# Factor rows, normalised rows and blocks of x in natural order of the contraction

## The chip, the cores and the metric

The kernel runs on one core of a Trainium2 chip. The metric is the device time of one execution in microseconds (us), as a median of runs. The engines are TensorE (PE, with its weight loads as PEld), VectorE (DVE), ScalarE (ACT), GpSimd (POOL) and SyncE (SP), whose queue issues nearly all DMAs.

## The reference

Eight sequences of 1024 tokens with 1024 features go through a cross attention over 64 memory rows and then a linear layer whose weight is a sum of eight factors; both have a layer norm before them and a residual.

```python
x = x + xattn(_layernorm(x), ctx)            # x: (8, 1024, 1024), ctx: (8, 64, 1024)
x = x + ffn(_layernorm(x), factors, bias)    # factors: (8, 1024, 1024), bias: (1024,)

scores = einsum('bsd,bmd->bsm', h, ctx) / sqrt(D)    # masked, then softmax over m
readout = einsum('bsm,bmd->bsd', attn, ctx)          # xattn
mixed = einsum('btd,rde->bte', h, factors)           # ffn
mixed = mixed / sqrt(8) + bias
```

All is float32.

## The kernel before

**Groups.** The 8192 tokens are cut into 16 groups of 512, each four row tiles of 128 tokens (`x` tiles, 128 x 1024). A group has two pairs of tiles; `q` and `h` number them, tile 2h + q.

**The weight.** The sum over the eight factors is made once, on TensorE. `load_stack e i c h` loads, for two of four blocks `j` of 256 rows of the weight, 16 rows of each of the 8 factors into a tile of 128 partitions: partition 8k + r holds row k of factor r, 4 KB long. A load is 512 KB; there are 64 of them, 33.5 MB, one for each `e` (4), `i` (2), `c` (2), `h` (2) and half tile `j`. `add_stack` multiplies them by a matrix `stack[i]` of 128 x 32 with a one where partition and output row belong together, so that the eight factors are summed; `i = 0` and `i = 1` are accumulated in one bank, each filling 16 of the 32 output rows of a block (line 718). `take_sums` copies the sums out of PSUM to the seven weight tiles `b11`, `t1` and so on, in chunks of 128 contraction rows numbered 2e + c (four to a tile; e and e + 2 go to different ones). `subtract_factors` and `combine_factors` make the further tiles of a Strassen-like scheme from them.

**The contraction order.** Chunk 2e + c of the 1024 features holds, from each of the four blocks `a` of 256, 32 of them. Before, a feature's index is read as (a, k, e, i, c) with k of 16, e of 4, i and c of 2: a chunk takes features with a step of 16 (over k) and a step of 2 (over i). The helpers `by_chunks`, `in_order` and `in_blocks` write that order as access patterns, and all that is contracted follows it:

- `normalize` (line 568) writes the normalised rows `h` from `x` with two activations of 512 elements, one for each c. In group 0 the result is in the order of chunks, in the others in blocks of 256 with the order inside each.
- `relayout` (line 585) moves, by 16 DMAs of 64 KB, block a of 32 tokens to partitions 32a and on, and `transpose_rows` (line 594) transposes that by squares of 32 x 32 on VectorE to `hT`, the stationary operand of the products. Group 0 is transposed on TensorE instead (`transpose_h_pe`).
- `load_blocks` (line 318) loads x a second time in such blocks, `transpose_blocks` (line 390) transposes them for the scores with two VectorE instructions of 128 x 256 for each e, one for each c. Groups 0 and 1 are transposed on TensorE (`transpose_x_pe`), with columns in steps of 8.
- `centre_memory` (line 287 and on) centres the memory rows, in the order of chunks with two activations, except for the first sequence.

**The products.** `product` (line 626) and `part` (line 676) are the matmuls of the linear layer, `give` (639) and `give_part` (690) add their results from PSUM to `x` on VectorE, `add_bias` (575) adds the bias on GpSimd, `read_out` (501) and `residual` (509) are the attention's output, `norm_sums` and `norm_squares` (537, 548) the statistics of the second norm. `store` (701) writes a tile out.

**Order.** Every engine works its instructions in the order in which the program writes them, and that is written by hand: the table START lists the steps of the beginning, among them all `load_stack` and `add_stack`, mixed with the work of groups 0 and 1; the table LOOP is then run for every group, with p, g, n and m standing for the group before, this one, the next and the one after. Tiles of the large kind come from ten buffers (`bigs`), taken and given back in the order of the table: factor loads, `xb`, `xT`, `h`, `hb` and `hT` share them. Eight PSUM banks are shared in the same manner. A factor load waits on SP's queue until the buffer that it takes has been given back by its reader, and whatever is behind it in SP's queue waits with it.

The load itself and the matrices that sum what it brings are these lines:

```python
src = factors.rearrange("r (j k e i c) n -> e i c j k r n", j=NA, e=NS, i=2, c=2)[e, i, c]
for j in range(2):
    nc.sync.dma_start(f[:, j], src[2 * h + j])
```

Of the kernel before, what the change touches and what calls it, by code (L numbers as in the profile page):

```python
# [10 lines left out]
F32 = mybir.dt.float32  # L11
BF16 = mybir.dt.bfloat16
AF = mybir.ActivationFunctionType
ALU = mybir.AluOpType
AX = mybir.AxisListType
# [91 lines left out]
def kernel(  # L107
# [17 lines left out]
    nc = tc.nc  # L125
    P = 128
    B, S, D = x.shape
    M = mem.shape[1]
    R = factors.shape[0]
    Q = 32  # L130
    NA = P // Q
    DA = D // NA
    NC = DA // Q
    KH = NC // 2
    NS = NC // 2
# [11 lines left out]
    const = ctx.enter_context(tc.tile_pool(name="const", bufs=1))  # L147
# [25 lines left out]
    ident = const.tile([P, P], F32, name="ident")  # L173
# [1 line left out]
    neghalf = const.tile([P, 4], F32, name="neghalf")  # L175
    nc.gpsimd.memset(neghalf, -0.5)

    stack = [const.tile([P, 2 * P // R], F32, name=f"stack{i}") for i in range(2)]
    for i in range(2):
        nc.vector.memset(stack[i], 0.0)  # L180
        nc.vector.tensor_reduce(
            stack[i].rearrange("p (k i) -> p i k", i=2)[:, i], ident.rearrange("p (k r) -> p k r", r=R), AX.X, ALU.add
        )

# [47 lines left out]

    st = {}

    def by_chunks(ap):

        return ap.rearrange("p (k e i c) -> p e c k i", e=NC // 2, i=2, c=2)

    def in_order(ap):
        return ap.rearrange("p (e c k i) -> p e c k i", e=NC // 2, c=2, i=2)

    def in_blocks(ap):

        return ap.rearrange("p (a e c k i) -> p e c a k i", a=NA, e=NC // 2, c=2, i=2)

    def constants():

        room = bigs.take("mask", [P, 2, 8 * P], "mask_room")  # L250
        st["mask"] = room[:, 0, : B * M].bitcast(mask.dtype)[:, : B * M], room[:, 1, : B * M], room[:B, 0, 4 * P : 5 * P]
        nc.scalar.dma_start(st["mask"][0], mask.rearrange("b m -> (b m)").partition_broadcast(P))
        for h in range(P // M):
            nc.scalar.dma_start(mask8[:, h], mask)
# [25 lines left out]
    def centre_memory(g: int):  # L280


        b = g // GPB
        m = st["mem", b]
        mc = bigs.take(("memc", b), [P, 2 * D], f"memc_{b}")[:, :D]
        msum = small.tile([P, 1], F32, tag="msum", name=f"msum_{b}")
        nc.scalar.activation(mc[:M], m[:M], AF.Copy, accum_out=msum[:M])
        mneg = small.tile([P, 1], F32, tag="mneg", name=f"mneg_{b}")
        nc.gpsimd.tensor_scalar_mul(mneg[:M], msum[:M], -1.0 / D)
        if b == 0:  # L290
            nc.scalar.activation(mc[:M], m[:M], AF.Identity, bias=mneg[:M])
        for c in range(2 if b else 0):
            nc.scalar.activation(
                in_order(mc)[:M, :, c], by_chunks(m)[:M, :, c], AF.Identity, bias=mneg[:M]
            )
        st["memc", b] = mc

# [85 lines left out]
    def transpose_blocks(g: int, h: int, e: int):  # L383

        xb = st["xb", g, h]
        if e == 0:
            st["xT", g, h] = bigs.take(("xT", g, h), [P, NC, 8 * Q], f"xT_{g}_{h}")
        xT = st["xT", g, h]
        for c in range(2):
            nc.vector.transpose(  # L390
                xT[:, 2 * e + c].rearrange("p (t j) -> p t j", j=Q),
                xb.rearrange("p t (k e i c) -> p e c t k i", e=NC // 2, i=2, c=2)[:, e, c],
            )
        if e == NC // 2 - 1:
            bigs.back(("xb", g, h))

# [160 lines left out]
    def normalize(g: int, q: int, h: int):  # L557
        rstd, nb = st["norm", g, q]
        if h == 0:
            st["h", g, q] = bigs.take(("h", g, q), [P, 2, D], f"h_{g}_{q}")  # L560
        src, dst = st["x", g, 2 * h + q], st["h", g, q][:, h, :]
        for c in range(2):
            fr = by_chunks(src)[:, :, c]
            if g == 0:
                to = in_order(dst)[:, :, c]
            else:
                to, fr = in_blocks(dst)[:, :, c], fr.rearrange("p e (a k) i -> p e a k i", a=NA)
            nc.scalar.activation(  # L568
                to, fr, AF.Identity, bias=nb[:, h : h + 1], scale=rstd[:, h : h + 1]
            )  # L570

    def add_bias(g: int, q: int, k: int, eng=nc.gpsimd):

# [131 lines left out]
    def load_stack(e: int, i: int, c: int, h: int):  # L705

        f = st["f", e, i, c, h] = bigs.take(("f", e, i, c, h), [P, 2, D], f"f_{e}_{i}_{c}_{h}")
        src = factors.rearrange("r (j k e i c) n -> e i c j k r n", j=NA, e=NS, i=2, c=2)[e, i, c]
        for j in range(2):
            nc.sync.dma_start(f[:, j], src[2 * h + j])  # L710

# [104 lines left out]
```

## Time and profile before

| | us |
|---|---|
| median of 3 runs | 1001.92 (1001.43 to 1004.05) |
| the profiled execution | 998.04 |
| its span, first to last instruction | 996.1 |
| TensorE busy | 937.4 |
| VectorE busy | 729.6 |
| ScalarE busy | 463.4 |
| GpSimd busy | 248.4 |

The profile is of one execution. Busy times are the time in which an engine runs at least one instruction; a mean duration times a count can be more, as instructions overlap. A line of the waits says who waited for whom, how long in total, how often, and the longest. A line of the groups says line, engine, operation, output and inputs, shapes and count, then busy time and the mean duration in ns, then the idle time before and what ended it. The DMA share of a window is the mean busy share of the 16 DMA engines.

### The profile page before, as it was taken

Reading aid. Unit: us, or ns where it says so; the run is one execution under the profiler, and the core shown is the slowest. Engines: PE = TensorE matmul, PEld = TensorE weight load, DVE = VectorE, ACT = ScalarE, POOL = GpSimd, SP = SyncE. Lnnn points to the kernel's source line nnn. Section 1 sums busy time; section 2 is a strip of 40 time slices with the busy share of each in tenths; the row PEclk is TensorE's granted clock in tenths of the full one; section 3 lists DMA queues with packets and bytes.
Section 4 is the critical chain, followed back from the end, with each engine's and each line's share of the span. In section 5 each row is a group of like instructions: output and inputs, shape, how many; then the busy total and the mean of one; then the engine's idle time right before and its main releaser. Section 6 shows DMA issues by size and latency. Waiting matters only on the chain.

```text
span 996.1 us, 12006 instructions
## 1 busy us (share of the span) xinstructions
PE 937.4 (94%) x3785; PEld 578.0 (58%) x3785; DVE 729.6 (73%) x1565; ACT 463.4 (47%) x848; POOL 248.4 (25%) x355
## 2 busy tenths in 40 slices
PE   5777766999999999999999999999999999999998
PEld 4322221566666666657575667665666757576666
DVE  4412143978797979797978889697979697888785
ACT  4745000167373727454655537363746456454200
POOL 0100020025141413223242313150423324232321
PEclk9979889999999999999999999999999999999999
DMA  9998899674847465565747484747565574742312
GB/s 277 255 269 225 205 224 234 149 191 141 197 148 167 138 166 159 167 151 161 188 135 198 127 191 151 176 140 164 155 171 148 155 189 135 193 131 77 105 69 85
DMA packets 98175, 167.07 MB, mean 168 GB/s; under 512 B 12864, under 2 KB 72384, under 8 KB 98112
## 3 DMA queue, kind: packets, MB, share of 16 engines
q1 hardware_dynamic: 97632, 165.20, 63.3%
q10 hardware_dynamic: 480, 1.12, 0.4%
q8 instruction: 29, 0.48, 0.2%
q14 instruction: 34, 0.28, 0.1%
HBM read 101.25 MB, written 33.55 MB: 135 GB/s over the span
## 4 chain that ended last, share of the span: by engine, by line
PE 80%; DMA 14%; SPq 3%; DVE 1%; issue 1%; ACT 0%; ACTq 0%; DVEq 0%
PE yu L626 30%; DMA f<-in_L_ffn_factors_dram 12%; PE ro L501 6%; PE y4u L676 5%; PE scT L433 5%; PE y3u L676 5%; PE y2u L676 5%; PE y5u L676 5%; SPq L585 3%; PE y4v L676 3%; PE y5v L676 3%; PE y3v L676 3%; PE y2v L676 3%; PE sum L718 2%; PE y3z L676 1%; PE y2z L676 1%
## 5 line engine op out<-in xcount | busy, mean ns | idle before, releaser
L575 POOL TENSOR_TENSOR x<-x,bias_bc 128x512 f32<-128x512 f32 x128 | 168.1, 1327 | 274.4 <-DVE x L639 209.5
L626 PE MATMUL yu<-b,hT 128*128 128x512 f32 x256 | 117.4, 602 | 10.0 <-DVE hT L594 8.2
L537 ACT ACTIVATE junkz<-x 128x1024 bf16<-128x1024 f32 x64 | 67.7, 1058 | 119.9 <-DVE x L509 117.1
L626 PE MATMUL yu<-t,hT 128*128 128x512 f32 x256 | 115.1, 592 | 0.0
L626 PE MATMUL yu<-t,s 128*128 128x512 f32 x256 | 115.0, 592 | 0.0
L594 DVE STREAM_TRANSPOSE hT<-hb 128x1024 f32<-128x1024 f32 x60 | 74.0, 1235 | 54.8 <-DMA hb<-h 50.8
L509 DVE SCALAR_TENSOR_TENSOR x<-ro,rden,x 128x512 f32<-128x512 f32 x128 | 89.9, 746 | 32.8 <-PE ro L501 32.8
L568 ACT ACTIVATE h<-x,nb,rstd 128x512 f32<-128x512 f32 x128 | 95.8, 820 | 16.2 <-PE sum L718 11.9
L364 ACT ACTIVATE junk<-x,nmean 128x1024 bf16<-128x1024 f32 x56 | 64.3, 1148 | 47.7 <-POOL nmean L335 46.7
L639 DVE SCALAR_TENSOR_TENSOR x<-yu,x 128x512 f32<-128x512 f32 x128 | 82.7, 677 | 5.0 <-PE yu L626 5.0
L626 PEld LDWEIGHTS yu<-b,hT 128*128 128x128 f32 x256 | 49.1, 193 | 61.8 <-issue 46.8
L718 PE MATMUL sum<-f,stack 128*32 128x512 f32 x256 | 57.1, 687 | 27.4 <-DMA f<-in_L_ffn_factors_dram 27.4
L390 DVE STREAM_TRANSPOSE xT<-xb 128x256 f32<-128x256 f32 x224 | 80.7, 417 | 1.2 <-issue 1.2
L626 PEld LDWEIGHTS yu<-t,s 128*128 128x128 f32 x256 | 48.5, 190 | 48.9 <-issue 46.8
L548 ACT ACTIVATE junky<-x,zm 128x1024 bf16<-128x1024 f32 x64 | 73.5, 1148 | 7.1 <-POOL zm L335 4.8
L626 PEld LDWEIGHTS yu<-t,hT 128*128 128x128 f32 x256 | 48.6, 190 | 47.6 <-issue 45.9
L501 PE MATMUL ro<-mem,eT 64*128 64x512 f32 x256 | 66.4, 628 | 2.6 <-ACT eT L490 2.6
L335 POOL TENSOR_SCALAR zm<-zs 128x2 f32<-128x2 f32 x28 | 6.3, 225 | 240.2 <-ACT junkz L537 240.2
L352 ACT ACTIVATE junk<-x 128x1024 bf16<-128x1024 f32 x56 | 59.0, 1053 | 13.4 <-DMA x<-in_x_dram 12.4
L690 DVE SCALAR_TENSOR_TENSOR x<-y3u,x 128x256 f32<-128x256 f32 x64 | 26.6, 416 | 47.3 <-PE y3u L676 44.3
L433 PE MATMUL scT<-xT,memT 128*64 128x256 f32 x512 | 58.8, 382 | 0.7 <-ACT memT L309 0.7
L718 PEld LDWEIGHTS sum<-f,stack 128*32 128x32 f32 x256 | 10.4, 118 | 70.1 <-DMA f<-in_L_ffn_factors_dram 44.9
(147 smaller groups left out, 1598.3 us busy)
## 6 DMA issues: line engine op xcount, KB each, us to landing
x<-in_x_dram SPq DMA_DIRECT2D x64, 512.0 KB, 4.1
f<-in_L_ffn_factors_dram SPq DMA_DIRECT2D x64, 512.0 KB, 13.8
out_dram<-x SPq DMA_DIRECT2D x64, 512.0 KB, 3.2
hb<-h SPq DMA_DIRECT2D x480, 64.0 KB, 2.0
xb<-in_x_dram SPq DMA_DIRECT2D x112, 256.0 KB, 7.1
mem<-in_ctx_dram SPq DMA_DIRECT2D x14, 256.0 KB, 5.4
mem<-in_ctx_dram ACTq DMA_DIRECT2D x2, 256.0 KB, 6.1
bias_bc<-in_L_ffn_bias_dram ACTq DMA_DIRECT2D x1, 512.0 KB
```

What stands on the lines that cost most here:

```text
L390: nc.vector.transpose(xT[:, 2 * e + c].rearrange("p (t j) -> p t j", j=Q), xb.rearrange("p t (k e i c) -> p e c t k i", e=NC // 2, i=2, c= ...
L433: nc.tensor.matmul(ps[ts(h, M), : 2 * P], mT[:, c, :], st["xT", g, h][:, c, :], start=(c == 0), stop=(c == NC - 1),)
L501: nc.tensor.matmul(ps, eT[ts(h, M), q, :], m[ts(h, M), ts(n, H)], start=True, stop=True)
L509: nc.vector.scalar_tensor_tensor(xt, st.pop(("ro", g, q, n, h)), rden[:, k : k + 1], xt, ALU.mult, ALU.add)
L548: nc.scalar.activation(junk, st["x", g, 2 * h + q], AF.Square, bias=nmean[:, h : h + 1], accum_out=ss[:, h : h + 1])
L568: nc.scalar.activation(to, fr, AF.Identity, bias=nb[:, h : h + 1], scale=rstd[:, h : h + 1])
L575: eng.tensor_add(xt, xt, bias_bc[:, ts(k % 2, H)])
L594: nc.vector.transpose(st["hT", g, q][:, h].rearrange("p c (t j) -> p t c j", j=Q), hb[:, h].rearrange("p t (c i) -> p t c i", i=Q),)
L626: nc.tensor.matmul(ps, lhs[:, c, :], wq[right][:, c, :], start=(first and c == 0), stop=(c == KH - 1), skip_group_check=True,)
L639: nc.vector.scalar_tensor_tensor(xt, st["y", g, q, key], ISR, xt, ALU.mult, ALU.add)
L676: nc.tensor.matmul(ps, lhs[:, c, :], right[:, c, :], start=(first and c == 0), stop=(c == 1), skip_group_check=True,)
L718: nc.tensor.matmul(st["sums", e, c][n][ts(j, Q)], stack[i], st["f", e, i, c, j // 2][:, j % 2, ts(n, H)], start=(i == 0), stop=(i == 1),)
```

## The change

The contraction is put in natural order: chunk 2e + c takes 32 consecutive features from each block of 256. A feature's index is read as (a, e, c, i, k), k innermost. A factor load then takes 16 consecutive rows of each of the 8 factors instead of 16 rows that are 16 apart; rows of the same factor lie next to each other in memory, those of different factors 4 MiB apart as before. `normalize` becomes one activation of 1024 elements (with the order of chunks written for group 0 alone), `transpose_blocks` one VectorE instruction of 128 x 512 for both c, `centre_memory` one activation. The two matrices `stack[0]` and `stack[1]` become two views of one tile of 48 columns, 16 columns apart. The tables START and LOOP are not touched, nor are tile sizes and buffers.

```diff
-    stack = [const.tile([P, 2 * P // R], F32, name=f"stack{i}") for i in range(2)]
-    for i in range(2):
-        nc.vector.memset(stack[i], 0.0)
-        nc.vector.tensor_reduce(
-            stack[i].rearrange("p (k i) -> p i k", i=2)[:, i], ident.rearrange("p (k r) -> p k r", r=R), AX.X, ALU.add
-        )
+    stacks = const.tile([P, 3 * P // R], F32, name="stacks")
+    nc.vector.memset(stacks, 0.0)
+    stack = [stacks[:, (1 - i) * P // R : (3 - i) * P // R] for i in range(2)]
+    nc.vector.tensor_reduce(stack[0][:, : P // R], ident.rearrange("p (k r) -> p k r", r=R), AX.X, ALU.add)
...
-        for c in range(2 if b else 0):
+        else:
             nc.scalar.activation(
-                in_order(mc)[:M, :, c], by_chunks(m)[:M, :, c], AF.Identity, bias=mneg[:M]
+                mc[:M].rearrange("p (n a w) -> p n a w", a=NA, w=Q),
+                m[:M].rearrange("p (a n w) -> p n a w", a=NA, w=Q),
+                AF.Identity,
+                bias=mneg[:M],
             )
...
-        for c in range(2):
-            nc.vector.transpose(
-                xT[:, 2 * e + c].rearrange("p (t j) -> p t j", j=Q),
-                xb.rearrange("p t (k e i c) -> p e c t k i", e=NC // 2, i=2, c=2)[:, e, c],
-            )
+        nc.vector.transpose(
+            xT[:, ts(e, 2)].rearrange("p c (t j) -> p t c j", j=Q),
+            xb[:, :, ts(e, 2 * Q)].rearrange("p t (c w) -> p t c w", w=Q),
+        )
...
-        for c in range(2):
-            fr = by_chunks(src)[:, :, c]
-            if g == 0:
-                to = in_order(dst)[:, :, c]
-            else:
-                to, fr = in_blocks(dst)[:, :, c], fr.rearrange("p e (a k) i -> p e a k i", a=NA)
-            nc.scalar.activation(
-                to, fr, AF.Identity, bias=nb[:, h : h + 1], scale=rstd[:, h : h + 1]
-            )
+        if g == 0:
+            dst = dst.rearrange("p (n a w) -> p a n w", n=NC, a=NA)
+            src = src.rearrange("p (a n w) -> p a n w", n=NC, a=NA)
+        nc.scalar.activation(dst, src, AF.Identity, bias=nb[:, h : h + 1], scale=rstd[:, h : h + 1])
...
-        src = factors.rearrange("r (j k e i c) n -> e i c j k r n", j=NA, e=NS, i=2, c=2)[e, i, c]
+        src = factors.rearrange("r (j e c i k) n -> e i c j k r n", j=NA, e=NS, i=2, c=2)[e, i, c]
```

More of the change, by code (lines that the diff above doesn't have):

```diff
@@ L235 @@
     st = {}
[L237 to L246, printed above, removed]
     def constants():
```

## The prediction

> **What bounds the kernel now.** I read the page first (busy time, the 40 slices, the chain of work that ended last), then the DMA shares by window, then the waits of TensorE, then the groups of the lines that the diff touches.
>
> ```profile
> span 996.1 us, 12006 instructions
> PE 937.4 (94%) x3785; PEld 578.0 (58%) x3785; DVE 729.6 (73%) x1565; ACT 463.4 (47%) x848; POOL 248.4 (25%) x355
> ...
> PE   5777766999999999999999999999999999999998
> ...
> PE 80%; DMA 14%; SPq 3%; DVE 1%; issue 1%; ACT 0%; ACTq 0%; DVEq 0%
> ```
>
> TensorE is idle for 996.1 - 937.4 = 58.7 us, and the slices show where: each is 25 us, and only the first seven or eight and the last are below 9. From 200 us on it is the bound. The chain has DMA as its second term, ACT and DVE with nearly nothing.
>
> The windows (length, then busy time of PE, PEld, DVE, ACT, POOL, the granted clock, the DMA share, GB/s) tell the two kinds of load apart:
>
> ```profile
> 2.00:4.00 2.00, 0.00 (x0) 0.00 (x0) 0.00 (x0) 0.38 (x1) 0.00 (x0) 1.00 0.98 363
> 10.00:12.00 2.00, 2.00 (x11) 2.00 (x10) 1.97 (x5) 0.88 (x2) 0.00 (x0) 1.00 1.02 416
> 60.00:70.00 10.00, 9.14 (x56) 3.96 (x48) 2.26 (x4) 6.31 (x12) 0.00 (x0) 0.88 1.03 268
> 150.00:160.00 10.00, 6.50 (x18) 1.69 (x18) 0.00 (x0) 0.58 (x1) 1.11 (x1) 0.83 1.03 239
> 250.00:300.00 50.00, 49.51 (x207) 32.46 (x206) 43.15 (x94) 27.97 (x52) 14.07 (x21) 1.00 0.65 171
> ```
>
> Before about 12 us the queue holds rows of x: 128 consecutive rows of 4 KB in each load (the first factor load is issued at 9.1 us behind six of them). They go at 363 to 416 GB/s. From then on it holds factor loads, of the same 4 KB pieces, and with the engines just as full (share 1.03) they bring 269, 268, 266 at 50 to 80 us and 239, 239, 240 at 140 to 170 us, mean 253.5. So the size of the pieces is not what makes them slow; the addresses are what differs. By the shapes, the 128 pieces of a factor load come from 8 factors, 4 MiB apart, and in each from 16 rows, 64 KiB apart.
>
> ```profile
> by line: PE yu L626 30.0%; DMA f<-in_L_ffn_factors_dram 12.3%; PE ro L501 5.8%; PE y4u L676 5.4%; PE scT L433 5.1%; PE y3u L676 5.1%; PE y2u L676 5.1%; PE y5u L676 4.9%; SPq L585 2.8%; PE y4v L676 2.7%; PE y5v L676 2.7%; PE y3v L676 2.7%; P
> ...
> PE sum L718 <- DMA f<-in_L_ffn_factors_dram: 27.4, 20, 3.9
> PE tp L405 <- DMA x<-in_x_dram: 10.9, 2, 9.7
> PE yu L626 <- DVE hT L594: 8.2, 1, 8.2
> PE ro L501 <- ACT eT L490: 2.6, 1, 2.6
> PE yu L626 <- ACT b L733: 1.8, 1, 1.8
> ```
>
> Factor loads carry 12.3% of the chain, 0.123 x 996.1 = 122.5 us, all before 172 us, and are the longest wait of TensorE. The start is bound by them; the rest by TensorE.
>
> **The loads.** The bytes (64 issues of 512 KB), the piece (4 KB) and the issues stay; the 16 rows of a factor become neighbours, 64 KB in one run, while the 8 factors stay 4 MiB apart. The trace has no such pattern; its neighbours are x (one run of 512 KB) and the factor loads of before. Upper end: they become like x at its best, 416 / 253.5 = 1.64 times the rate. Lower end: the same step the other way, 253.5 / 1.64 = 155 GB/s, since one can't exclude from the trace that the 64 KiB steps are what keeps the eight factors' rows out of each other's way. Other factors' rows are still mixed into each load, so I don't take x's full rate but the geometric middle between it and no change, 1.28 times (325 GB/s). The 122.5 us then shrink by 122.5 x (1 - 1/1.28) = 26.8 us. Not all arrives: faster loads expose what runs beside them. In the start TensorE waits 27.4 us for factors, and 8.2 + 2.6 + 1.8 = 12.6 us for things that don't get faster (the transposed rows behind the two relayouts, each 16 issues on SP's queue at some 0.6 us; the softmax weights; the copied sums), and factor loads need one of ten buffers that TensorE frees. I take 27.4 / 40.0 = 0.7 of it: 19 us.
>
> [...]
>
> **The normalised rows.** Before, two activations of 512 per tile, each with strided reads:
>
> ```profile
> L568 ACT ACTIVATE h<-x,nb,rstd 128x512 f32<-128x512 f32 x128 | 95.8, 820 | 16.2 <-PE sum L718 11.9 <-POOL nb L554 4.4
> L548 ACT ACTIVATE junky<-x,zm 128x1024 bf16<-128x1024 f32 x64 | 73.5, 1148 | 7.1 <-POOL zm L335 4.8
> L390 DVE STREAM_TRANSPOSE xT<-xb 128x256 f32<-128x256 f32 x224 | 80.7, 417 | 1.2 <-issue 1.2
> L594 DVE STREAM_TRANSPOSE hT<-hb 128x1024 f32<-128x1024 f32 x60 | 74.0, 1235 | 54.8 <-DMA hb<-h 50.8 <-issue 2.0 <-PE memTp L306 2.0
> ```
>
> After, 64 of 1024. Nearest is the square's pass over 1024 with a bias, 1148 ns (1058 for the sum's pass, at most 2 x 820 = 1640): 64 x 1.15 = 73 us against 128 x 0.82 = 105, some 32 us less in durations, 22 less in busy time. Beside TensorE it is worth nothing: its windows add up to 53.4 us of idle time before 200 us, so 5.3 of the 58.7 come later, 4.6 of these in the last 46 us, where ACT does nothing. On the path it counts in the start alone, where group 1's four activations (2.95 us) stand ahead of a relayout; two take 2.3. Two such places give 1.3 us at most; I take 1. Group 0's rows, in four tiles, write runs of 32 elements instead; between 1148 and 1640 ns that is no loss against 1640.
>
> **The transposes of x.** 224 of 256 elements become 112 of 512. A line through 417 ns at 256 and 1235 at 1024 gives 690 at 512 (bounds: half of 1235, 618, and twice 417, 834): 112 x 0.69 = 77 us instead of 93, 16 us off DVE. What hides it is the same: after 200 us TensorE never waits for DVE for more than the 0.8 and 0.7 us of combined rows. If that cover were thinner the longer single instruction could delay an eviction by 0.27 us; the products' banks show no such wait, so nothing is counted.
>
> **The rest.** The centred memory rows lose one activation in each of seven batches: hidden under TensorE, nothing. The stack matrices lose one memset and one reduce (0.09 + 0.29 us on DVE before 2 us, where DVE waits for x until 9.6): nothing. The matrices are still 32 columns wide, slid along a common tile, so all 256 sum matmuls stay; TensorE loses and gains no instruction. No wait is added and no issue is moved past another: the tables START and LOOP are the same.
>
> **Sum.** The profiled execution took 998.04 us, 996.1 of span and 1.9 around it: 998.0 - 19 - 1 = 978. The median, 1001.92, lies 3.9 above that execution, so 982 as a median. At x's rate: 47.8 x 0.7 = 33.5, so 967.
>
> **The rivals.** *The factors' 4 MiB sets the rate.* The loads stay near 250 GB/s, and what remains is the 1 us of activations: 1001 us. For it: both 8 factors and 64 KiB separate the loads from x, and only the second goes. Against it: the rate was not one number (268 at 60 us, 239 at 150), with the same factor distance in every load, so something else in the addresses matters too.
>
> *Neighbouring rows of eight factors get in each other's way.* Place: the factor loads from 13 to 172 us. [...] If that costs as much as I expect it to bring, the rate is 253.5 / 1.28 = 198 GB/s, the 122.5 us grow by 34, nothing hides them because they are the chain already, and the median becomes 1035; with the full step 122.5 x 0.64 = 78, 1079. It decides as soon as the rate falls under 247 GB/s (3 us more on the chain). For it: the only measured pattern with several factors is slow. Against it: x shows that neighbouring rows as such are fast.
>
> *A faster load that gives nothing.* If buffers and relayouts held the start fully, the DMA share would be well under 1 there. It is 1.02 to 1.04 in nearly every window to 170 us except 90 to 110 and 120 to 130 (0.60 to 0.82), so this can only eat a part, the 0.3 already taken off.
>
> **How the numbers follow.** Faster loads 0.52, no effect on them 0.09, slower loads 0.39: the rows of x speak for the first, that the loads keep the factors' distance leaves much room for the last. About 0.3% (3 us) is what a measurement of this kernel can tell from no change, so the same three chances stand for faster, same and slower. The forecast is the likeliest case, 982; its own range is 964 to 996. To leave out no more than 2 in 10 the range must reach through no change into slower loads, past its middle at 1035: 962 to 1042.
>
> **What would show it.** Right: DMA windows of 300 GB/s or more at 50 to 80 us with a share of 1, the median time to landing of factor loads under 11 us (13.8 now), TensorE's wait for them at line 718 under half of 27.4 us, the last sum matmul near 150 us instead of 173. In any case: 64 activations near 1.15 us, 112 transposes near 0.69 us, and the stage from 200 us to the end as long as now. Wrong: windows at 250 or below, or a start that keeps its length with a lower DMA share, which would mean that buffers or relayouts took the place of the loads; or a longer stretch between 250 and 900 us, which would mean that the wider instructions hold up evictions.

## The result, and the profile after

The median of the changed kernel is 1006.18 us (20 runs, 998.05 to 1010.94) against 1001.83 us of before (20 runs): a ratio of 1.0059, interval 1.0034 to 1.0084. The forecast was 982. The kernel became slower by some 4 to 6 us (the medians lie 4.4 apart, the ratio makes 5.9) where 20 us less were forecast; the time lies within the stated range of 962 to 1042, on the slower side of no change. In a later comparison the same kernel (e10) stood at 1.0039 (1.0016 to 1.0061).

The page of the changed kernel; its profiled execution took 1004.66 us:

```profile
span 1002.9 us, 11821 instructions
PE 940.1 (94%) x3785; PEld 579.8 (58%) x3785; DVE 720.8 (72%) x1451; ACT 441.5 (44%) x777; POOL 250.8 (25%) x355
...
PE   5767757999999999999999999999999999999998
```

ACT is 22 us less busy and DVE 9, and nothing came of it: TensorE's slices are full from the eighth on, as before. The windows of the same kernel, columns as in the prediction:

```profile
60.00:70.00 10.00, 9.77 (x48) 3.22 (x46) 0.00 (x0) 3.36 (x6) 0.00 (x0) 0.72 1.03 245
150.00:160.00 10.00, 6.33 (x31) 1.29 (x31) 2.57 (x5) 0.00 (x0) 5.36 (x4) 0.89 1.04 236
```

Where 300 GB/s or more were expected, the factor loads run at 245 and 236 with the DMA engines full (268 and 239 before). But a second profiled execution of the kernel before (e8) has, in the same two windows, the rates of the changed kernel:

```profile
60.00:70.00 10.00, 8.61 (x54) 3.74 (x46) 2.17 (x4) 6.25 (x11) 0.00 (x0) 0.89 1.04 247
150.00:160.00 10.00, 6.32 (x31) 1.18 (x21) 1.67 (x3) 0.09 (x1) 4.47 (x4) 0.89 1.03 233
```

So 268 against 245 is no measure of the change. TensorE's waits and the groups of the touched lines in the changed kernel:

```profile
PE sum L702 <- DMA f<-in_L_ffn_factors_dram: 29.7, 19, 4.5
PE yu L610 <- DVE hT L578: 11.2, 1, 11.2
```

```profile
L554 ACT ACTIVATE h<-x,nb,rstd 128x1024 f32<-128x1024 f32 x64 | 75.7, 1230 | 19.2 <-PE sum L702 14.2 <-POOL nb L543 5.0
L379 DVE STREAM_TRANSPOSE xT<-xb 128x512 f32<-128x512 f32 x112 | 73.5, 684 | 1.2 <-issue 1.2
```

The wait for factors is 29.7 us against 27.4 before, but 31.3 in e8; the one for transposed rows is 11.2 against 8.2. The merged instructions cost nearly what was worked out: 1230 ns (1148 taken) and 684 ns (690).

Where the time went is read from the sum matmuls of each kernel (their duration as min, median, max, then first and last start). Before, after, and before in a second profiled execution (e8):

```profile
L718 PE MATMUL sum<-f,stack x256: 589/592/1063, 33.6 to 173.4; 128*32 128x512 f32 x128
```

```profile
L702 PE MATMUL sum<-f,stacks x256: 589/593/1063, 33.9 to 179.2; 128*32 128x512 f32 x128
```

```profile
L718 PE MATMUL sum<-f,stack x256: 589/592/1062, 32.6 to 177.0; 128*32 128x512 f32 x128
```

From that last matmul to the end of the span it is 996.1 - 173.4 = 822.7, 1002.9 - 179.2 = 823.7 and 1000.0 - 177.0 = 823.0 us. All that differs by more than 1 us lies ahead of it, in the stage of the loads. And the start of one and the same program differs by 3.6 us between two executions, so the 6.8 us between the two profiled spans can't be explained line by line; the medians and their intervals must decide.

### The profile page after: what moved, and what is told of

It reads as the page before. It is cut to its first block, busy times and chain, and to the rows that moved or that the text cites. A ratio compares the mean times of both kernels' runs of the same rounds, so it can differ in the third digit from the quotient of the medians.

```text
span 1002.9 us, 11821 instructions
## 1 busy us (share of the span) xinstructions
PE 940.1 (94%) x3785; PEld 579.8 (58%) x3785; DVE 720.8 (72%) x1451; ACT 441.5 (44%) x777; POOL 250.8 (25%) x355
## 4 chain that ended last, share of the span: by engine, by line
PE 79%; DMA 15%; SPq 4%; DVE 1%; issue 1%; ACT 0%; ACTq 0%; DVEq 0%
PE yu L610 30%; DMA f<-in_L_ffn_factors_dram 13%; PE ro L490 6%; PE y4u L660 5%; PE scT L422 5%; PE y3u L660 5%; PE y2u L660 5%; PE y5u L660 5%; SPq L569 3%; PE y4v L660 3%; PE y5v L660 3%; PE y3v L660 3%; PE y2v L660 2%; PE sum L702 2%; PE y3z L660 1%; PE y2z L660 1%
## 5 line engine op out<-in xcount | busy, mean ns | idle before, releaser
L610 PE MATMUL yu<-b,hT 128*128 128x512 f32 x256 | 118.7, 608 | 13.0 <-DVE hT L578 11.2
L610 PEld LDWEIGHTS yu<-b,hT 128*128 128x128 f32 x256 | 49.7, 195 | 65.6 <-issue 47.8
L702 PE MATMUL sum<-f,stacks 128*32 128x512 f32 x256 | 57.7, 696 | 29.9 <-DMA f<-in_L_ffn_factors_dram 29.7
L554 ACT ACTIVATE h<-x,nb,rstd 128x1024 f32<-128x1024 f32 x64 | 75.7, 1230 | 19.2 <-PE sum L702 14.2
L354 ACT ACTIVATE junk<-x,nmean 128x1024 bf16<-128x1024 f32 x56 | 64.3, 1148 | 45.0 <-POOL nmean L325 44.1
L537 ACT ACTIVATE junky<-x,zm 128x1024 bf16<-128x1024 f32 x64 | 73.5, 1148 | 7.4 <-POOL zm L325 4.8
L379 DVE STREAM_TRANSPOSE xT<-xb 128x512 f32<-128x512 f32 x112 | 73.5, 684 | 1.2 <-issue 1.2
L702 PEld LDWEIGHTS sum<-f,stacks 128*32 128x32 f32 x256 | 10.2, 119 | 73.3 <-DMA f<-in_L_ffn_factors_dram 45.1
```

The costliest lines, as they stand in the source:

```text
L379: nc.vector.transpose(xT[:, ts(e, 2)].rearrange("p c (t j) -> p t c j", j=Q), xb[:, :, ts(e, 2 * Q)].rearrange("p t (c w) -> p t c w", w=Q),)
L537: nc.scalar.activation(junk, st["x", g, 2 * h + q], AF.Square, bias=nmean[:, h : h + 1], accum_out=ss[:, h : h + 1])
L554: nc.scalar.activation(dst, src, AF.Identity, bias=nb[:, h : h + 1], scale=rstd[:, h : h + 1])
L610: nc.tensor.matmul(ps, lhs[:, c, :], wq[right][:, c, :], start=(first and c == 0), stop=(c == KH - 1), skip_group_check=True,)
L702: nc.tensor.matmul(st["sums", e, c][n][ts(j, Q)], stack[i], st["f", e, i, c, j // 2][:, j % 2, ts(n, H)], start=(i == 0), stop=(i == 1),)
```

## The experiments

### What makes the factor loads slow

**e1, e5, e9, e18: loads alone.** Kernels that only load, 12 times 512 KB in a pattern, and one VectorE reduce after each pattern, which the next pattern's loads wait for.

```diff
+    for j, src in enumerate(srcs):            # 128 rows of 4 KB each
+        nc.sync.dma_start(room[:, j], src)
+    nc.vector.tensor_reduce(res[:, n : n + 1], room[:, :, 0], AX.X, ALU.add)
```

> Computes nothing of the reference: it only loads 12 x 512 KB of the factors in each of nine address patterns, one after the other, all in pieces of 4 KB to 128 partitions. What counts is the GB/s of each pattern at a full DMA share. Theory A (the 4 MiB from factor to factor set the rate, the order of the 16 rows hardly counts): 16 rows of 8 factors give 235 to 260 GB/s with rows 16 apart and with rows that are neighbours, the latter some 4% less; one factor alone gives 400 whether its 128 rows are neighbours or 8 apart; two and four factors lie between. Theory B (rows far apart are what is slow, in any number of factors): one factor with rows 8 apart falls to about 250 too. Theory C (the size of the piece or the SBUF side sets it): all nine at about 250.

> Computes nothing of the reference: 12 loads of 512 KB in each of 13 address patterns, one after the other. First 16 rows of 8 factors, 16 apart and neighbouring in turn, three times each. Theory A1 (the order of the rows costs the loads 3 to 4%): neighbouring rows 27.5 us against 26.5 in each of the three pairs. Theory A2 (it costs nothing): equal within 1%, the pairs of both signs. Then 16 neighbouring rows at 8 places 512 KiB, 1 MiB and 2 MiB apart; if only the 4 MiB from place to place is slow these give 400 GB/s; if eight places in any distance are slow they stay at 240. Then 32 rows of four factors: neighbouring, 32 rows apart, and every second factor (8 MiB apart); and 64 rows of two factors 16 MiB apart. If the distance of 4 MiB or more is slow by itself they fall to 240; if it is having eight places in one load, all are near 410.

> Computes nothing of the reference: 12 loads of 512 KB in each of 12 patterns (the last in 24 loads of 256 KB to 64 partitions). First 16 rows of 8 factors, neighbouring and 16 apart in turn, four times: if the order of rows costs the loads nothing, the means of the four differ by under 0.5%. Then loads with the same shape (16 times 8 pieces) inside one factor: 16 runs of 8 rows close together, and 16 neighbouring rows at 8 places 64 KiB apart. Theory D (the shape 16 x 8 of the load is slow, wherever the pieces lie): both at 230 GB/s. Theory E (pieces at eight far places are slow): the runs of 8 close rows at 380 or more; 64 KiB apart lies at either. 32 rows at 4 places 512 KiB apart: near 400 by both. 16 rows of four factors to 64 partitions: near 400 by E if it is the number of places, by D if the 8 is what counts; 230 if it is the 16.

> Computes nothing of the reference: 12 loads of 512 KB in each of 8 patterns, all inside one factor with the pieces close together: 16 runs of 8 rows, 32 runs of 4, 64 runs of 2 (one row left out after each run), then 128 rows without a gap; all twice. Theory D (the shape 16 x 8 of a load is slow wherever its pieces lie): 230 GB/s for the first and 360 to 390 for the others. Theory E (places in memory): all four alike, since all lie within 1 MiB.

Windows from the middle of patterns; the columns are length, DVE and POOL busy, clock, DMA share, GB/s. A load is named by the shape of its source: 16 x 8 is 16 rows of each of 8 places, with the 16 in the outer step. In e1: 16 x 8 with rows 16 apart, then neighbouring; 128 rows of one factor; 8 x 16 (the factor in the outer step) with neighbouring rows, then with rows 16 apart; 32 rows of 4 factors; 64 rows of 2:

```profile
10.00:25.00 15.00, 0.00 (x0) 0.00 (x0) 1.00 1.03 238
40.00:55.00 15.00, 0.00 (x0) 0.00 (x0) 1.00 1.03 241
65.00:75.00 10.00, 0.00 (x0) 0.00 (x0) 1.00 1.02 410
90.00:110.00 20.00, 0.00 (x0) 0.00 (x0) 1.00 0.51 210
120.00:155.00 35.00, 0.00 (x0) 0.00 (x0) 1.00 0.51 143
165.00:175.00 10.00, 0.00 (x0) 0.00 (x0) 1.00 1.01 410
185.00:195.00 10.00, 0.00 (x0) 0.00 (x0) 1.00 1.02 415
```

So four factors, 4 MiB apart like the eight, load at 410 GB/s, as fast as one. Theory A of e1 (the distance) falls, and so do its rivals: one factor with rows 8 apart gave 413 (B), and four of the nine patterns are at 410 and more (C). The pieces are the same in all nine: 128 rows of 4 KB in each load. In e5, 16 rows at eight places only 512 KiB, 1 and 2 MiB apart stayed at 233 to 235; four places 8 MiB apart gave 414, and with rows 32 apart 388. In e9, eight places 64 KiB apart inside one factor gave 231, and 16 runs of 8 rows lying next to each other, all within 576 KB, 242, where theory E wanted 380 or more. The last one, e18, holds all in one factor and close together: runs of 8 rows with one left out (a pattern of 16 x 8 pieces), of 4 (32 x 4), of 2 (64 x 2), and 128 rows in a row:

```profile
10.00:25.00 15.00, 0.00 (x0) 0.00 (x0) 1.00 1.03 250
35.00:45.00 10.00, 0.00 (x0) 0.00 (x0) 1.00 1.03 414
53.00:63.00 10.00, 0.00 (x0) 0.00 (x0) 1.00 0.96 370
71.00:81.00 10.00, 0.00 (x0) 0.00 (x0) 1.00 1.02 406
95.00:110.00 15.00, 0.00 (x0) 0.00 (x0) 1.00 1.03 242
122.00:132.00 10.00, 0.00 (x0) 0.00 (x0) 1.00 1.03 413
```

Theory D holds: a load written as 16 x 8 pieces to 128 partitions ran at 229 to 250 GB/s in every place tried, and one of 32 x 4 at 388 to 414. Eight factors in a load are slow because they make that shape, not because of where they are in memory. (Places can matter in another shape: the two loads of 8 x 16 in e1 differ in their rows' places alone, and with rows 16 apart the rate is 143 instead of 210.) Why the shape 16 x 8 is slow no run shows. e9's load of 16 x 4 pieces to 64 partitions gave 271, which neither theory had forecast. And e1's 8 x 16 with neighbouring rows, 210 GB/s at a share of 0.51, brings as much for each busy engine as 410 at 1.02 (25 to 26 GB/s, an estimate from these two rows, with 16 engines), where 16 x 8 brings some 15 (241 at 1.03).

The 4 MiB from factor to factor, which the prediction's first rival held to set the rate, does not explain it: eight places 4 MiB apart and 64 KiB apart load alike (229 to 247 over e1, e5, e9 and e16, and 231), and four places 4 MiB apart at 410.

### How much the loads are worth

**e4: one factor in each load.** Before, with

```diff
-        src = factors.rearrange("r (j k e i c) n -> e i c j k r n", j=NA, e=NS, i=2, c=2)[e, i, c]
+        src = factors.rearrange("(e i) (c h j p) n -> e i c h j p n", e=NS, i=2, c=2, h=2, j=2)[e, i, c]
+        src = [src[g, j] for g in range(2) for j in range(2)]
```

> The kernel before with every factor load taking 128 neighbouring rows of one factor (each byte of the factors is still loaded once; the sums are over rows and not over factors, so the output isn't the reference's). If the distance of the factors sets the rate and the start is bound by the loads: windows of 350 to 410 GB/s, and by the prediction's factor of 0.7 some 33 us less, 965 to 975. If buffers and relayouts hold the start: under 10 us less, with a DMA share well under 1 in the start.

957.48 us, ratio 0.954 (0.951 to 0.957): 45 us less, where the factor of 0.7 had given 33. Its windows:

```profile
30.00:40.00 10.00, 8.39 (x53) 2.61 (x52) 6.13 (x12) 8.18 (x20) 1.96 (x4) 1.00 1.03 411
60.00:70.00 10.00, 8.19 (x56) 2.28 (x49) 4.07 (x7) 8.37 (x15) 0.00 (x0) 1.00 0.90 310
80.00:90.00 10.00, 8.15 (x36) 2.37 (x36) 3.10 (x4) 0.43 (x1) 0.00 (x0) 1.00 1.00 366
```

So the start was bound by the loads as the prediction read it. The DMA share does fall under 1 in places (0.42 at 70 to 80 us, where TensorE is busy for 9.94 of 10 us); TensorE's wait for factors goes from 27.4 to 3.2 us.

**e6, e7: 32 rows of four factors.** The changed kernel (e6), and before with the same loads and its own activations and transposes (e7):

```diff
+    four = const.tile([P, Q], F32, name="stack")
+    nc.vector.tensor_reduce(four, ident.rearrange("p (k r) -> p k r", r=R // 2), AX.X, ALU.add)
+    stack = [four, four]
...
+        src = factors.rearrange("(s r) (j e c k) n -> e s c j k r n", s=2, j=NA, e=NS, c=2)[e, i, c]
```

> The changed kernel with each factor load taking 32 neighbouring rows of 4 factors instead of 16 rows of 8, and the two halves of the factors added in PSUM in place of the two halves of the rows. It computes the reference. If the eight factors in one load set the rate: loads at 350 to 410 GB/s, the start some 45 us shorter as with one factor per load, 955 to 962. If more than one factor in a load is already slow: 990 to 1006.

> The kernel before with the same loads of 32 neighbouring rows of 4 factors; activations and transposes stay in the old order, so the weight's rows stand in another order than the features (the output isn't the reference's). Beside e6 it shows what the wider instructions do when the loads are fast: if they cost 4 us, this is 4 us below e6; if they bring the 1 us of the prediction, 1 us above; the cost of loads of neighbouring rows is in both.

e6: 957.15 us, ratio 0.9585 (0.9523 to 0.9647). e7: 955.76, 0.9582 (0.9518 to 0.9646). Four factors are as good as one, and with fast loads no difference between wide and narrow instructions can be seen (e6 from 956.24 to 958.2, e7 from 954.81 to 959.07).

### Where the 4 us come from

**e2, e3, e12: the loads' row order alone, and all but it.** e2 is before with the new line of `load_stack`, e3 and e12 the changed kernel with the old one. The results of this part stand together in the table below.

> The kernel before with the addresses of the factor loads alone changed to 16 neighbouring rows; all else stays in the old order, so the weight's rows stand in another order than the features (the output isn't the reference's). Theory A (the neighbouring rows load some 4% slower, 122 us of chain x 0.035): +4 to +5 us, a ratio of 1.004 to 1.005, like the whole change. Rival (the wider activations and transposes cost, the loads' rate is the same): 1.000.

> The changed kernel with the addresses of the factor loads alone put back to rows 16 apart, so the weight's rows stand in another order than the features (the output isn't the reference's). Theory A: the wider instructions bring the 0 to 1 us of the prediction, 1.000 to 0.999. Rival: +4 us, 1.004, all of the change.

> As e3: the changed kernel with the factor loads' addresses 16 rows apart (the output isn't the reference's). Against e10 it gives the cost of the neighbouring rows in the kernel: by the pairs of e5 under 1 us, so within 0.2% of e10 and 1.001 to 1.006 of before; by the first comparison 4 us below e10.

**e8, e10: before and after once more.**

> The kernel before once more, for a second profile of it. If the length of the start differs between executions of one program (the loads' rate by the execution, and not by the program), the last sum matmul is not at 173 us again but up to 180, and from there to the end it is 822 to 824 us as in all the others.

> The changed kernel once more, beside e11 and e12 on one chip. Again 1.003 to 1.008 if the first comparison's difference is the program's.

**e11: narrow instructions.** The changed kernel with two activations and two transposes where it has one:

```diff
-        nc.scalar.activation(dst, src, AF.Identity, ...)
+        for c in range(2):
+            to, fr = (dst[:, ts(c, 2)], src[:, ts(c, 2)]) if g == 0 else (dst[:, ts(c, H)], src[:, ts(c, H)])
+            nc.scalar.activation(to, fr, AF.Identity, ...)
```

> The changed kernel with its normalised rows in two activations of 512 per tile again (halves of the row, read in order) and its transposes of x in two of 256. It computes the reference. If the wider instructions cost the time in the start, this is back at 1.000 to 1.002; if they cost nothing and the order does, it stays with e10, 1.003 to 1.007.

**e13, e14, e15, e17: the place of the tiles.** The common tile of the two matrices is 192 bytes per partition where two of 128 were, so everything allocated behind it stands 64 bytes lower: the factor tiles start 32 bytes over a multiple of 256 instead of 96 (worked out from the sizes of the tiles ahead of them). e13 takes that away, e14 puts it into before, e15 and e17 start the large tiles on a multiple of 256.

```diff
-    stacks = const.tile([P, 3 * P // R], F32, name="stacks")
+    stacks = const.tile([P, 4 * P // R], F32, name="stacks")         # e13
+    stacks = const.tile([P, 3 * P // R + 56], F32, name="stacks")    # e15
...
+    four = const.tile([P, Q + 8], F32, name="stack")[:, :Q]          # e17, otherwise as e6
...
-    stack = [const.tile([P, 2 * P // R], F32, name=f"stack{i}") for i in range(2)]
+    stack = [const.tile([P, 2 * P // R + 48 * i], F32, name=f"stack{i}")[:, : 2 * P // R] for i in range(2)]   # e14
```

> The changed kernel with the common tile of the two matrices widened from 48 to 64 columns (16 unused), so that all tiles behind it stand at the SBUF addresses of the kernel before; in the change they stand 64 bytes lower. It computes the reference. Theory P (the 64 bytes cost the loads a few per cent): back to 1.000 to 1.002 of before. Theory R (the row order costs it): stays at 1.004 to 1.005.

> The kernel before with 192 unused bytes behind its second matrix, so that all tiles behind stand at the changed kernel's place relative to multiples of 256 bytes (32 over one, instead of 96). It computes the reference. Theory P: 1.003 to 1.005 of before, like the change. Theory R: 1.000.

> The changed kernel with its common tile widened by 224 bytes, so that the factor tiles start on a multiple of 256 bytes. It computes the reference. Theory P: no slower than e13, perhaps faster by some per cent of the loads' time, 0.995 to 1.002. Theory R: 1.004 to 1.005.

> The changed kernel with loads of 32 neighbouring rows of 4 factors (as e6) and 32 unused bytes behind the matrix, so that the large tiles start on a multiple of 256 bytes. It computes the reference. If the place of the tiles matters for any load: 2 to 4 us under e6, 953 to 956; if only the slow loads of 16 x 8 pieces feel it: as e6, 956 to 958, 0.955.

| kernel | row order of the loads | bytes over 256 | instructions | ratio to before | interval |
|---|---|---|---|---|---|
| after, first | near | 32 | wide | 1.0059 | 1.0034 to 1.0084 |
| after, again (e10) | near | 32 | wide | 1.0039 | 1.0016 to 1.0061 |
| e11 | near | 32 | narrow | 1.0045 | 1.0026 to 1.0064 |
| e3 | 16 apart | 32 | wide | 1.0014 | 0.9992 to 1.0036 |
| e12 | 16 apart | 32 | wide | 1.0039 | 1.0011 to 1.0066 |
| e14 | 16 apart | 32 | narrow | 1.0013 | 0.9992 to 1.0035 |
| e2 | near | 96 | narrow | 1.0010 | 0.9990 to 1.0031 |
| e13 | near | 96 | wide | 1.0020 | 1.0002 to 1.0037 |
| e15 | near | 0 | wide | 0.9958 | 0.9931 to 0.9985 |

No theory gets all of its forecasts. The row order alone (e2) does not bring the 1.004 of theory A, nor does all but the order in e3, though its repeat e12 does; and e12 stands where e10 stands (medians 1004.70 and 1005.39 us), so in that comparison the row order is worth under 1 us. Taking the 64 bytes away (e13) brings the time down as theory P said, putting them into before (e14) does not bring it up to 1.003.

**e16: place and order by themselves.**

> Computes nothing of the reference: 12 loads of 512 KB in each of 14 patterns. 16 neighbouring rows of 8 factors to tiles that start 96, 32 and 0 bytes over a multiple of 256, three times in turn; then rows 16 apart at 96 and 32; then 128 rows of one factor at 96, 32 and 0. Theory P: at 32 slower than at 96 by 3 to 4% in each of the three turns (1 us of 27). Theory R: the three alike, and the rows 16 apart faster by 3% than the neighbouring ones at the same place.

The reduces after each pattern (start, duration): the difference of two starts is the time of a pattern. The first nine are neighbouring rows at 96, 32 and 0 bytes over 256, three times in turn; then rows 16 apart at 96 and at 32.

```profile
30.79 0.17 DVE L47 TENSOR_REDUCE res<-room 128x1 f32<-128x12 f32 x1 [28.87 <-DMA room<-in_L_ffn_factors_dram]
60.59 0.17 DVE L47 TENSOR_REDUCE res<-room 128x1 f32<-128x12 f32 x1 [29.63 <-DMA room<-in_L_ffn_factors_dram]
89.97 0.17 DVE L47 TENSOR_REDUCE res<-room 128x1 f32<-128x12 f32 x1 [29.21 <-DMA room<-in_L_ffn_factors_dram]
119.75 0.17 DVE L47 TENSOR_REDUCE res<-room 128x1 f32<-128x12 f32 x1 [29.60 <-DMA room<-in_L_ffn_factors_dram]
150.19 0.17 DVE L47 TENSOR_REDUCE res<-room 128x1 f32<-128x12 f32 x1 [30.27 <-DMA room<-in_L_ffn_factors_dram]
179.26 0.17 DVE L47 TENSOR_REDUCE res<-room 128x1 f32<-128x12 f32 x1 [28.90 <-DMA room<-in_L_ffn_factors_dram]
209.10 0.17 DVE L47 TENSOR_REDUCE res<-room 128x1 f32<-128x12 f32 x1 [29.67 <-DMA room<-in_L_ffn_factors_dram]
239.21 0.17 DVE L47 TENSOR_REDUCE res<-room 128x1 f32<-128x12 f32 x1 [29.93 <-DMA room<-in_L_ffn_factors_dram]
268.70 0.17 DVE L47 TENSOR_REDUCE res<-room 128x1 f32<-128x12 f32 x1 [29.32 <-DMA room<-in_L_ffn_factors_dram]
297.52 0.17 DVE L47 TENSOR_REDUCE res<-room 128x1 f32<-128x12 f32 x1 [28.65 <-DMA room<-in_L_ffn_factors_dram]
326.92 0.17 DVE L47 TENSOR_REDUCE res<-room 128x1 f32<-128x12 f32 x1 [29.22 <-DMA room<-in_L_ffn_factors_dram]
```

Neighbouring rows: at 96 bytes 29.78 and 29.84 us (the very first has the start in it), at 32 bytes 29.80, 30.44 and 30.11, at 0 bytes 29.38, 29.07 and 29.49. Means 29.81, 30.12, 29.31: 32 is 1.0% slower than 96, 0 is 1.7% faster. Theory P had 3 to 4% between 32 and 96, and one of the three turns at 32 (29.80) is as fast as those at 96; the three at 0 are below all others. The rows of one factor at the end of e16, measured once each, come in the same order: 18.60 at 96, 18.79 at 32, 17.99 at 0. Rows 16 apart: 28.82 at 96 and 29.40 at 32, 3.3% and 2.4% faster than neighbouring ones at the same place. But the order's part isn't steady: without each first pattern, e5's pairs gave 29.57 (neighbouring) against 29.49, 0.3%, and e9's 30.24 against 29.27, 3.3%.

What follows, with 122.5 us of chain: the row order costs 0.3 to 3.3%, 0.4 to 4 us; the 64 bytes some 1%, 1.2 us. Both point the slow way, and both together make the measured 4 to 6 us at the upper end. In the kernel, each alone (e2 and e14) is not told from nothing, e13 just is, and only kernels with the tiles 32 bytes over and one more of the changes stand clear above 1, and of the two measurements of one such kernel (e3 and e12) only one does. The wider instructions are not the main cause: taken back (e11), the time stays within the intervals. How the 4 us divide between order and place stays open, since a start differs by as much from execution to execution.

e15 is the other side: on a multiple of 256 bytes the changed kernel falls to 999.54 us, 0.9958 (0.9931 to 0.9985), below before. The loads alone explain 1.7 to 2.7% of 122.5, 2 to 3 us; it is some 4 us under e13 in the same comparison, with executions from 988.47 to 1003.76 us, and the rest isn't explained. Why 0 is the fastest of the three places no run shows.

**The best version, e17**, joins both: 32 rows of four factors and tiles on a multiple of 256 bytes. 953.4 us (951.92 to 955.96), ratio 0.9536 (0.9504 to 0.9567), where e6 had 956.24 to 958.2. The two stand in different comparisons and their ratios' intervals overlap, so the 3 to 4 us are likely the place of the tiles but not shown to be. Its last sum matmul starts 50 us earlier than the changed kernel's:

```profile
L701 PE MATMUL sum<-f,stack x256: 592/593/1062, 32.3 to 128.8; 128*32 128x512 f32 x128
```

## Why the prediction was wrong

**The bound: right.** The start is bound by the factor loads (45 us less with those of e4), the rest by TensorE (in the changed kernel busy for 50.00 of the 50 us from 500 to 550). From the last sum matmul to the end, the profiled executions of before (two), after, e2, e3, e4, e6, e11, e13, e15 and e17 took 821.6 to 823.7 us, whatever was done to ACT and DVE.

**The step that failed** is "So the size of the pieces is not what makes them slow; the addresses are what differs." Two things differ between x's loads and the factors': the addresses, and the shape in which the load is written, 128 rows in one step against 16 x 8 in two. The prediction gives the 8 factors and 16 rows, but reads them as distances alone. From that came the term of 1.28 times the rate, 325 GB/s and 19 us. The change leaves the shape, and the rate stayed too: 235 to 261 GB/s where the DMA engines are full, and by the loads alone a factor of 0.97 to 1 for the order. Even the 253.5 GB/s that the sum starts from is one execution's: the same six windows of e8 give 244 on average.

**The rival that came true** in its sign, slower loads, was priced at 34 us from the same false step and had a chance of 0.39; the rival of unchanged loads (1001 us, 0.09) was nearest in time and in rate, with a reason that is also refuted: four factors 4 MiB apart load at 410 GB/s. That the sign was among the rivals, and the time within a range that reached to 1042 for this rival's sake, is luck as far as the mechanism goes: neither its price nor its reason was borne out. A change that leaves the load's shape alone should have had its largest chance near no change.

**The 0.7 of the gain that would arrive: too low.** At x's rate 47.8 x 0.7 = 33.5 us were reckoned; with loads at that rate (e4) it was 45 of 47.8, 0.95. The relayouts and buffers that I set against it do show as a DMA share below 1 (0.42 at 70 to 80 us of e4), but TensorE has other work there (busy for 9.94 of those 10 us).

**The rest of the sum: right in the main.** 1230 and 684 ns against 1148 and 690; both hidden, as reckoned. The 1 us credited for faster activations ahead of relayouts is not visible.

**What was not in the sum at all** is the 64 bytes: "The stack matrices lose one memset and one reduce" looked at instructions alone. The same edit moved every later tile, by the loads alone some 1% or 1.2 us, which is not clear of the scatter.

## What to carry to other kernels

A load's access pattern is more than a list of addresses: before reordering rows, time the same bytes in another shape (32 x 4 instead of 16 x 8), by a kernel of loads alone; here that separates 240 from 410 GB/s and is worth 45 us where the loads bound the start. When a small constant tile changes its size, look at where the large tiles behind it now begin. And when a program's start varies by some us from execution to execution, one profile each of before and after can't explain a difference of that size.

## What the runs showed of the hardware that was not expected

- In the kernels of loads alone, 128 pieces of 4 KB to 128 partitions ran, written as 16 x 8, at 229 to 250 GB/s in every place tried, as 32 x 4, 64 x 2 or 128 at 370 to 415, all with the DMA engines busy at a share near 1.
- With 8 pieces outermost (8 x 16) the share was 0.51, with 4 (4 x 32) 0.26 and 105 GB/s, as if only half and a quarter of the 16 DMA engines had work; no view shows the engines one by one. In 8 x 16 the rows' places counted too: 210 GB/s with neighbouring rows, 143 with rows 16 apart.
- The same loads of 16 x 8 took 29.31, 30.12 and 29.81 us (means of 3, 3 and 2) with tiles 0, 32 and 96 bytes over a multiple of 256; the last two overlap in their single values.
- Two executions of one program differed by 3.6 us in the end of the stage that the loads bind (173.4 and 177.0 us).
